# Layer 0's projections through the values' bank, and a reordered last stage, in a two-layer transformer kernel

## The chip, the cores and the metric

The kernel runs on one core of a Trainium2 chip. The metric is the device time of one execution in microseconds. A core has five engines that run their own instruction streams in order and meet through semaphores: TensorE (PE; its weight loads are shown apart as PEld), VectorE (DVE), ScalarE (ACT), GpSimd (POOL) and SyncE (SP). SP mostly issues DMAs; its queue, too, is worked in order. PSUM, into which TensorE writes, has eight banks of 128 x 512 floats.

## The reference

Two sequences of 1024 tokens with 128 features pass through two layers, all in 32-bit floats:

```python
x = x + L0_attn(layernorm(x))   # 16 heads of 64; q, k, v = z @ w @ fc + bias; softmax(q k / 8) v; out projection
x = x + L0_ffn(layernorm(x))    # 8 experts, top 2 by softmax of the router, silu(h1) * h2
x = x + L1_attn(layernorm(x))   # 16 heads of 8 with a shared rotary part of 32, causal
x = x + L1_ffn(layernorm(x))    # shared expert + 8 experts (512 wide), top 2 of a small router net
```

Layer 0's q is `(z @ wq @ fcq_w + fcq_b) / 8`, its k is `z @ wk @ fck_w + fck_b`.

## The kernel before

**PSUM.** One set of pools serves the whole kernel: two wide tiles of two banks for scores (ps_s, `wide()`), three single banks in rotation for transposes and everything else (ps_t, `bank()`), and one bank for the sums of attention values (ps_a, `acc_bank()`). A new tile of a pool waits until the last reader of the tile that had its bank is done.

**Layer 0's attention** (L387 to L640). Its order on TensorE, VectorE and ScalarE is written out by hand. The work is cut in 128 units: batch, pair of heads, block of 128 queries (eight blocks, `qt` 0 to 7, for each pair). The loop at L600 runs three units deep. In step i TensorE computes the scores of unit i (L501, four matmuls, the two heads on the two halves of the rows), transposes the probabilities of the first head of unit i-1 (L551, into two banks), adds the values of unit i-2 into ps_a (L568), and transposes the second head of unit i-1. VectorE takes maxima and moves scores to SBUF (L510), copies ps_a out when four units are summed (L575, at qt 1 and 5 of the loop), and evicts the second head's transposes (L557). ScalarE evicts the first head's transposes (L557) and takes the exponentials (L520). At qt 1 the row sums of the finished pair are transposed (L532), sent through HBM to spread them over the partitions (L538, L540, SP's queue), and GpSimd scales the outputs (L542).

The next pair's q and k are projected by `project_qk` (L473) in two halves of 512 tokens, at qt 2 and 4: two matmuls into two banks of ps_t, q evicted by VectorE (L486), k by ScalarE (L488). In steps where no projection stands and qt isn't 1, one step of other work may run: batch 1's latents, the folding of the output weights, later the routing of layer 0's experts.

At the start batch 0's layernorm runs: statistics on VectorE (L128, L129), a square root on ScalarE (L134), a reciprocal (L135) and the scaling (L153) on VectorE, then transposes, latents (L430, L435) and the first two projections. The biases bq, bk and bv are loaded by L401 on SP's queue, after x; each is 128 x 8 floats that lie apart in HBM.

**Layer 1's experts** (L897). For each batch the tokens are sorted by expert into tiles of 128 (23 tiles for batch 0; 21 for batch 1, whose last 128 tokens go through all experts). `experts1` fetches the tokens of a tile with an indirect DMA seven tiles ahead (L907), loads expert weights of 256 KB on SP's queue into four buffers (L894, issued four tiles ahead of use), and then per tile: L946 (up matmuls), L880 and L888 on VectorE with a tanh on ScalarE (L883) between them, L954 (down matmuls), L962, a scaling by the gate (L937), and an indirect store to `results` (L938). `combine1` (L1004) loads a batch's results (`z`, four DMAs on SP, L1011), which wait for all scatters of the batch, and four steps later adds them to x (L1018) and stores x.

**The last stage** (L1264 to L1284) is a list of loops over generators. When layer 1's attention is done, seven steps of batch 1's routing and sorting are left (`side`: L280 to L375 with the matmuls L289, L357, L363), eleven steps of batch 0's `experts1`, the shared expert on batch 1's first half (`half`, L1038 and L1049), and `rest` (the routing of the last token tile, L829 to L859, then the shared expert on the second half). Each loop takes one step of some of them in turn.

Of the kernel before, what the change touches and what calls it, by code (L numbers as in the profile page):

```python
# [51 lines left out]
def two_layers(ctx, tc, a, out):  # L52
# [15 lines left out]
    def bank():  # L68
        return psum["t"].tile([P, QB], F32, tag="t", name="ps_t")
# [4 lines left out]
    def load(pool, name, shape, src, eng):  # L74
        t = pool.tile(list(shape), F32, tag=name, name=name)
        eng.dma_start(out=t if len(src.shape) == 2 else t.rearrange("p (a b) -> p a b", b=src.shape[-1])
                      if len(shape) == 2 else t, in_=src)
        return t
# [308 lines left out]
    with ExitStack() as st:  # L387
# [12 lines left out]
        for k in "qkv":  # L400
            bias[k] = load(w0, f"b{k}", [P, NP], a[f"fc{k}"][D0:D0 + 1, :].rearrange("o (j p) -> p (o j)", p=P),  # L401
                           nc.sync)
        fco = load(w0, "fco", [P, NP, C], a["fco_w"].rearrange("(j p) c -> p j c", p=P), nc.scalar)
        fco_b = load(w0, "fco_b", [1, C], a["fco_b"], nc.scalar)

# [67 lines left out]
        def project_qk(b, pr, n):  # L473

            if n == 0:
                qk = a0.tile([P, 2, T], F32, tag="qk", name="qk", bufs=2)
                pairs[b, pr] = qk
            qk = pairs[b, pr]
            z, cols = lat[b][0], slice(n * QB, (n + 1) * QB)
            got = []  # L480
            for h in range(2):
                ps = bank()
                rows = slice(h * D0, (h + 1) * D0)
                nc.tensor.matmul(ps, fcqk[rows, pr * P:(pr + 1) * P], z[rows, cols], start=True, stop=True)  # L484
                got.append(ps)
            nc.vector.tensor_scalar(qk[:, 0, cols], got[0], bias["q"][:, pr:pr + 1], 1.0 / math.sqrt(D0),  # L486
                                    ALU.add, ALU.mult)
            nc.scalar.activation(qk[:, 1, cols], got[1], AF.Identity, bias=bias["k"][:, pr:pr + 1])  # L488

        units = [(b, pr, qt) for b in range(NB) for pr in range(NP) for qt in range(NT)]  # L490
        N = len(units)
# [96 lines left out]
        with tc.manual_schedule(engines={ET.PE, ET.DVE, ET.Activation}):  # L588
            lat = {}
            for _ in latents(0):  # L590
                pass
            project_qk(0, 0, 0)
            project_qk(0, 0, 1)
            wout = w0.tile([P, NP, C], F32, tag="wout", name="wout")
            extra = [latents(1), output_weights()]
            routing = route0(0, f0w, "lnT", 1, routed0[0], 1)
            temp = [lambda: a0.tile([P, T], F32, tag="pT", name="h0", bufs=6)[:, :QB],
                    lambda: a0.tile([P, T], F32, tag="p", name="o0", bufs=4)[:, :QB]]
            experts = experts0(0, routed0[0], temp)
            for i in range(N + 3):  # L600
                s = scores(i) if i < N else None
                if 1 <= i <= N:
                    probsT[i - 1] = [a0.tile([P, NT, P], F32, tag="pT", name="pT", bufs=6) for _ in range(2)]
                    evict(i - 1, 0, fill(i - 1, 0), nc.scalar.copy)
                if i < N:
                    exponentials(i, [maximum(s[0]), maximum(s[1])])
                done = units[i - 2][:2] if i >= NT and i % NT == 1 else None
                if done:
                    rs = reciprocals(done)
                if 2 <= i <= N + 1:  # L610
                    values(i - 2)
                if 1 <= i <= N:
                    evict(i - 1, 1, fill(i - 1, 1), nc.vector.tensor_copy)
                    del probs[i - 1]
                if i >= N:
                    if i == N + 1:
                        scale(done, rs)
                        for t0 in (0, TPB):
                            project_out(NB - 1, t0, TPB, range(NP - 1))
                    experts(i < N + 2)  # L620
                    continue
                b, pr, qt = units[i]
                after = (b, pr + 1) if pr + 1 < NP else (b + 1, 0)
                if after[0] < NB and qt in (2, 4):
                    project_qk(*after, qt // 2 - 1)
                if done:
                    scale(done, rs)
                if b == 0 and pr and qt not in (1, 2, 4) and extra:
                    if next(extra[0], N) == N:
                        extra.pop(0)  # L630
                        if not extra:
                            obias = output_bias()
                            for bb in range(NB):
                                nc.gpsimd.tensor_tensor(xs[bb], xs[bb], bc(obias.unsqueeze(1), [P, NT, C]), ALU.add)
                if (b, pr) == (1, 1):
                    project_out(0, qt, 1, range(NP))
                if b == 1 and pr > 1 and qt not in (1, 2, 4):
                    next(routing, None)
            for t0 in (0, TPB):
                project_out(NB - 1, t0, TPB, [NP - 1])  # L640
# [360 lines left out]
        rows = slice(t0 * P, (t0 + nt) * P)  # L1001
        nc.sync.dma_start(out=out[b, rows, :].rearrange("(t p) c -> p t c", p=P), in_=xs[b][:, t0:t0 + nt, :])

    def combine1(b, nt):  # L1004

        z = a1.tile([P, 2, NT, C], F32, tag="pT", name="z", bufs=2)
        groups = [(t0, min(TPB, nt - t0)) for t0 in range(0, nt, TPB)]
        for t0, n in groups:
            for k in range(2):
                rows = k * T + t0 * P  # L1010
                nc.sync.dma_start(out=z[:, k, t0:t0 + n], in_=results[b][rows:rows + n * P, :].rearrange("(t p) c -> p t c", p=P))  # L1011
        for _ in range(4):
            yield
        for t0, n in groups:
            yield
            xv = xs[b][:, t0:t0 + n, :]
            for k in range(2):
                nc.vector.tensor_tensor(xv, z[:, k, t0:t0 + n], xv, ALU.add)  # L1018
            store(b, t0, n)
# [34 lines left out]
    with ExitStack():  # L1054
# [122 lines left out]
        with tc.manual_schedule(engines={ET.PE, ET.DVE, ET.Activation, ET.Pool}):  # L1177
# [81 lines left out]
            def run(*steps):  # L1259

                return any([next(g, N) is None for g in steps])


            half, rest = shared1(1, 0), chain(route1(1, NT - 1, 1, "k0", "k1"), shared1(1, 1))  # L1264
            while side:
                work(N)
                run(experts) or run(half)
                run(rest)
            after = experts1(1, NT - 1, 1)
            for _ in range(AHEAD):  # L1270
                run(after)
                run(experts) or run(half) or run(rest)
            while run(experts):
                run(after)
            combining = combine1(0, NT)
            while run(after):
                run(half) or run(rest)
                run(combining)
            while run(half) or run(rest):
                pass  # L1280
            dense, combining = all_experts1(1, NT - 1), combine1(1, NT - 1)
            while run(combining, dense):
                pass
            store(1, NT - 1, 1)  # L1284
# [69 lines left out]
```

## Time and profile before

| | us |
|---|---|
| median of three runs | 1495.02 (1491.14 to 1495.07) |
| the profiled execution | 1490.81 |
| its span, first to last instruction | 1489.0 |
| busy: TensorE | 1393.7 |
| busy: VectorE | 1066.2 |
| busy: ScalarE | 885.2 |
| busy: GpSimd | 269.8 |
| L501, scores of layer 0, 1024 matmul passes | 279.9 |
| L568, values of layer 0, 4096 passes | 251.9 |
| L510, maxima of layer 0 | 303.3 |
| L520, exponentials of layer 0 | 293.1 |

A row of the timeline reads: start, length, engine, line, operation, output<-input, shape, count; in brackets the idle time of the engine just before and what ended it. A row of the waits reads: engine, its waiting instruction <- what released it: total us, times, longest us. In the slices (40 equal parts of the span, 37.2 us each) a digit is a busy share in tenths. Two TensorE passes make one matmul in 32-bit floats.

### The profile page before, as it was taken

What the parts mean: (1) busy time and instruction counts of PE and PEld (TensorE: products, weight loads), DVE (VectorE), ACT (ScalarE), POOL (GpSimd) and SP (SyncE); (2) the same over time, 40 slices, a digit from 0 to 9 for tenths busy, and PEclk for the clock granted to TensorE, in tenths of its full rate; (3) what the DMA queues carried; (4) which work ended last, traced back from release to release, by engine and by line L of the source; (5) the groups of instructions that cost most, each with busy time, mean ns of one, the idle gap of its engine ahead of it and who ended that gap; (6) DMA issues with size and microseconds to landing.
All of it is one profiled execution on the core that took longest, in us unless ns stands there. A gap on an engine that the chain in (4) does not pass through costs nothing.

```text
span 1489.0 us, 40492 instructions
## 1 busy us (share of the span) xinstructions
PE 1393.7 (94%) x16930; PEld 987.7 (66%) x16930; DVE 1066.2 (72%) x2375; ACT 885.2 (59%) x1864; POOL 269.8 (18%) x246
## 2 busy tenths in 40 slices
PE   6999999999999999999998978999988899988797
PEld 3776677777777667767765555666655567767686
DVE  4777767777766876877646558767888767878576
ACT  4667666666654676666513346876755677763443
POOL 1010001000000000000053561002111211222663
PEclk9999999999999999999999989999988999999999
DMA  4000000000000000000020030000000101112454
GB/s 110 2 16 16 16 16 9 9 16 17 16 16 1 17 16 17 16 17 4 15 49 0 1 90 2 2 2 2 2 9 9 42 25 35 47 38 53 137 135 118
DMA packets 34391, 43.15 MB, mean 29 GB/s; under 512 B 10641, under 2 KB 22578, under 8 KB 34210
## 3 DMA queue, kind: packets, MB, share of 16 engines
q1 hardware_dynamic: 28288, 28.47, 7.0%
q0 software_dynamic: 4352, 10.70, 2.7%
q8 instruction: 134, 2.20, 0.6%
q10 hardware_dynamic: 1570, 1.41, 0.4%
q14 instruction: 47, 0.39, 0.1%
HBM read 35.51 MB, written 5.05 MB: 27 GB/s over the span
## 4 chain that ended last, share of the span: by engine, by line
PE 77%; DVE 12%; ACT 6%; issue 3%; DMA 1%; POOL 0%; ACTq 0%; DVEq 0%; POOLq 0%
PE ps_a L568 16%; PE ps_s L501 15%; PE ps_t L551 10%; PE ps_s L1076 8%; PE ps_t L484 4%; PE ps_t L1118 4%; PE ps_s L253 3%; PE ps_a L1158 3%; DVE ps_s L1084 2%; PE ps_t L583 2%; ACT p L1106 2%; PE ps_t L954 2%; PE ps_t L714 2%; PE ps_t L946 1%; PE ps_t L263 1%
## 5 line engine op out<-in xcount | busy, mean ns | idle before, releaser
L510 DVE CUSTOM_DVE_ANT_0 p<-ps_s,zero 128x1024 f32<-128x1024 f32 x256 | 303.3, 1222 | 104.7 <-PE ps_s L501 104.7
L520 ACT ACTIVATE p<-p,nmx 128x1024 f32<-128x1024 f32 x256 | 293.1, 1153 | 3.0 <-DVE nmx L510 2.9
L501 PE MATMUL ps_s<-qk 64*128 64x512 f32 x1024 | 279.9, 609 | 1.5 <-DVE nmx L510 1.4
L557 ACT COPY pT<-ps_t 128x512 f32<-128x512 f32 x256 | 137.5, 589 | 211.2 <-PE ps_t L551 211.2
L568 PE MATMUL ps_a<-pT,zv 128*64 128x128 f32 x4096 | 251.9, 276 | 0.0
L551 PEld LDWEIGHTS ps_t<-ident,p 64*128 64x128 f32 x4096 | 168.1, 138 | 89.9 <-issue 86.0
L568 PEld LDWEIGHTS ps_a<-pT,zv 128*64 128x64 f32 x4096 | 221.0, 137 | 9.3 <-issue 0.8
L557 DVE COPY pT<-ps_t 128x512 f32<-128x512 f32 x256 | 164.7, 685 | 65.0 <-PE ps_t L551 65.0
L551 PE MATMUL ps_t<-ident,p 64*128 64x64 f32 x4096 | 193.7, 226 | 1.3 <-DVE pT L557 0.7
L1076 PE MATMUL ps_s<-k,qm 64*128 64x512 f32 (+3 forms) x768 | 171.2, 534 | 17.3 <-ACT p L1106 12.4
L1084 DVE CUSTOM_DVE_ANT_0 p<-ps_s,cmask 128x640 f32<-128x640 f32 (+3 forms) x128 | 125.9, 1021 | 64.8 <-PE ps_s L1076 55.6
L501 PEld LDWEIGHTS ps_s<-qk 64*128 64x128 f32 x1024 | 100.3, 188 | 84.8 <-issue 75.0
L542 POOL TENSOR_TENSOR aoT<-aoT,recip 128x1024 f32<-128x1024 f32 x16 | 37.8, 2363 | 647.2 <-DMA recip<-flat 594.2
L1118 PEld LDWEIGHTS ps_t<-ident,p 64*128 64x128 f32 x2304 | 104.1, 142 | 48.1 <-issue 23.3
L1124 ACT COPY pT<-ps_t 128x512 f32<-128x512 f32 (+3 forms) x192 | 95.9, 534 | 63.2 <-PE ps_t L1118 62.2
L1106 ACT ACTIVATE p<-p,nmx 128x640 f32<-128x640 f32 (+3 forms) x128 | 125.9, 992 | 4.3 <-DVE nmx L1084 4.2
L1076 PEld LDWEIGHTS ps_s<-k,qm 64*128 64x128 f32 x768 | 71.8, 194 | 83.4 <-issue 40.5
L1118 PE MATMUL ps_t<-ident,p 64*128 64x64 f32 x2304 | 118.0, 230 | 3.1 <-ACT pT L1124 1.3
L1158 PE MATMUL ps_a<-pT,vx 128*32 128x128 f32 x2304 | 100.0, 283 | 7.6 <-DVE pT L1124 7.5
L1124 DVE COPY pT<-ps_t 128x128 f32<-128x128 f32 (+3 forms) x192 | 87.2, 482 | 2.6 <-PE ps_t L1118 2.0
L1106 ACT ACTIVATE p<-ps_s,nmx 128x128 f32<-128x128 f32 (+3 forms) x128 | 66.5, 526 | 27.9 <-DVE nmx L1084 27.6
L1084 DVE CUSTOM_DVE_ANT_0 ps_s<-ps_s,cmask 128x128 f32<-128x128 f32 (+3 forms) x128 | 63.6, 498 | 24.7 <-PE ps_s L1076 19.9
(245 smaller groups left out, 1779.1 us busy)
## 6 DMA issues: line engine op xcount, KB each, us to landing
we<-in_we SPq DMA_DIRECT2D x52, 256.0 KB, 2.7
recip<-flat SPq DMA_DIRECT2D x32, 256.0 KB, 3.9
we<-in_we POOLq DMA_DIRECT2D x1, 2048.0 KB
z<-results SPq DMA_DIRECT2D x6, 256.0 KB, 4.0
x<-in_x SPq DMA_DIRECT2D x4, 256.0 KB, 3.9
up<-in_up_proj POOLq DMA_DIRECT2D x1, 1024.0 KB, 12.1
normed<-y SPq DMA_DIRECT2D x3, 256.0 KB, 2.3
out_x<-x SPq DMA_DIRECT2D x3, 256.0 KB
```

Source lines behind the costliest of these rows:

```text
L501: nc.tensor.matmul(s[h][:, n * QB:(n + 1) * QB], qk[rows, 0, qt * P:(qt + 1) * P], qk[rows, 1, n * QB:(n + 1) * QB], start=True, stop=True)
L510: nc.vector.tensor_tensor_reduce(p, s, bc(zero, [P, T]), -1.0, 3e38, ALU.add, ALU.min, nmx)
L520: nc.scalar.activation(p, p, AF.Exp, bias=nmx, scale=-1.0, accum_out=ssum[:, h, qt:qt + 1])
L551: nc.tensor.transpose(ps[r][:, k * 64:(k + 1) * 64], probs[i][h][rows, k * P:(k + 1) * P], ident[rows, rows])
L557: copy(probsT[i][h][:, :, r * 64:(r + 1) * 64], ps[r].rearrange("p (j q) -> p j q", q=64))
L568: nc.tensor.matmul(acc[h * D0:(h + 1) * D0, cols], zv[:, j, :], probsT[i][h][:, j, :], start=(j == 0), stop=(j == NT - 1))
L1076: nc.tensor.matmul(s[h][:, n * QB:n * QB + w], qms[b, qt][rows, pr, :], kTs[b][pr // 4][rows, n * QB:n * QB + w], start=True, stop=True)
L1084: nc.vector.tensor_tensor_reduce(to[:, :nk], s[:, :nk], cmask[:, T - nk:], -1.0, 3e38, ALU.add, ALU.min, nmx)
L1106: nc.scalar.activation(p[:, h, :nk], s[h][:, :nk], AF.Exp, bias=nmx[h], scale=-1.0, accum_out=sums[b, qt][:, head:head + 1])
L1118: nc.tensor.transpose(ps[r][:, c * 64:(c + 1) * 64], probs[i][rows, h, j * P:(j + 1) * P], ident[rows, rows])
L1124: copy(probsT[i][:, 8 * f:8 * f + n, r * 64:(r + 1) * 64], ps[r][:, :n * 64].rearrange("p (j q) -> p j q", q=64))
L1158: nc.tensor.matmul(acc[to * 32:(to + 1) * 32, k * P:(k + 1) * P], vx[:, j, g, pr % 4 * 24:pr % 4 * 24 + 32], probsT[i][:, h * (qt + 1) + j ...
```

## The change

The change has three parts. `project_qk` puts q into ps_a and k into ps_t, both evictions go to ScalarE (q's with the scale 1/8 as an immediate and a bias that is scaled once at the start, `scaled_bq`), and projections stand at qt 1 and 5, so that other work may use six of eight steps. `combine1` can wait a number of steps before it loads. In the last stage, the loop over `side` takes a step of batch 0's experts only every second time and no step of `half`; the loop of seven fetches alternates `half` and batch 0's experts; batch 0's last experts then alternate with batch 1's first steps; and batch 0's combining waits six steps.

```diff
+        scaled_bq = w0.tile([P, NP], F32, tag="scaled_bq", name="scaled_bq")
+        nc.vector.tensor_scalar(scaled_bq, bias["q"], 1.0 / math.sqrt(D0), None, ALU.mult)
         fco = load(w0, "fco", [P, NP, C], a["fco_w"].rearrange("(j p) c -> p j c", p=P), nc.scalar)
...
-            got = []
+            got = [acc_bank(), bank()]
             for h in range(2):
-                ps = bank()
                 rows = slice(h * D0, (h + 1) * D0)
-                nc.tensor.matmul(ps, fcqk[rows, pr * P:(pr + 1) * P], z[rows, cols], start=True, stop=True)
-                got.append(ps)
-            nc.vector.tensor_scalar(qk[:, 0, cols], got[0], bias["q"][:, pr:pr + 1], 1.0 / math.sqrt(D0),
-                                    ALU.add, ALU.mult)
-            nc.scalar.activation(qk[:, 1, cols], got[1], AF.Identity, bias=bias["k"][:, pr:pr + 1])
+                nc.tensor.matmul(got[h], fcqk[rows, pr * P:(pr + 1) * P], z[rows, cols], start=True, stop=True)
+            for h, (scale, add) in enumerate(((1.0 / math.sqrt(D0), scaled_bq), (1.0, bias["k"]))):
+                nc.scalar.activation(qk[:, h, cols], got[h], AF.Identity, bias=add[:, pr:pr + 1], scale=scale)
...
-                if after[0] < NB and qt in (2, 4):
-                    project_qk(*after, qt // 2 - 1)
+                if after[0] < NB and qt in (1, 5):
+                    project_qk(*after, qt // TPB)
                 if done:
                     scale(done, rs)
-                if b == 0 and pr and qt not in (1, 2, 4) and extra:
+                if b == 0 and pr and qt not in (1, 5) and extra:
...
-                if b == 1 and pr > 1 and qt not in (1, 2, 4):
+                if b == 1 and pr > 1 and qt not in (1, 5):
                     next(routing, None)
...
-    def combine1(b, nt):
+    def combine1(b, nt, wait):
+        for _ in range(wait):
+            yield
         z = a1.tile([P, 2, NT, C], F32, tag="pT", name="z", bufs=2)
...
+            k = 0
             while side:
                 work(N)
-                run(experts) or run(half)
+                if k % 2 == 0:
+                    run(experts)
                 run(rest)
+                k += 1
             after = experts1(1, NT - 1, 1)
-            for _ in range(AHEAD):
+            for k in range(AHEAD):
                 run(after)
-                run(experts) or run(half) or run(rest)
+                run(half) if k % 2 else run(experts)
             while run(experts):
                 run(after)
-            combining = combine1(0, NT)
+            combining = combine1(0, NT, 6)
             while run(after):
                 run(half) or run(rest)
                 run(combining)
             while run(half) or run(rest):
                 pass
-            dense, combining = all_experts1(1, NT - 1), combine1(1, NT - 1)
+            dense, combining = all_experts1(1, NT - 1), combine1(1, NT - 1, 0)
```

## The prediction

> **What bounds the kernel now.** I read the page's first two parts first, to see which engine is full in which stage.
>
> ```profile
> PE 1393.7 (94%) x16930; PEld 987.7 (66%) x16930; DVE 1066.2 (72%) x2375; ACT 885.2 (59%) x1864; POOL 269.8 (18%) x246
> PE   6999999999999999999998978999988899988797
> PEclk9999999999999999999999989999988999999999
> ```
>
> Layer 0's attention fills the first half: TensorE is in the nines, at full clock. A microsecond taken from TensorE's order there should come off the end. The 37th slice shows a hole (7). Next, one unit without and one with a projection, from the timeline:
>
> ```profile
> 206.35 1.97 PE L568 MATMUL ps_a<-pT,zv 128*64 128x128 f32 x32
> 208.25 0.71 PE L551 MATMUL ps_t<-ident,p 64*128 64x64 f32 x16
> 208.53 0.63 DVE L575 COPY aoT<-ps_a 128x512 f32<-128x512 f32 x1
> 208.88 0.28 PE L532 MATMUL ps_t<-ident,rs 128*16 128x128 f32 x1
> 209.07 1.27 DVE L557 COPY pT<-ps_t 128x512 f32<-128x512 f32 x2
> ...
> 211.50 1.97 PE L568 MATMUL ps_a<-pT,zv 128*64 128x128 f32 x32
> 213.88 0.30 PEld L484 LDWEIGHTS ps_t<-zqk,fcqk 64*128 64x128 f32 x2
> 214.14 1.29 DVE L557 COPY pT<-ps_t 128x512 f32<-128x512 f32 x2 [0.54 <-PE ps_t L551]
> 214.88 0.18 PEld L484 LDWEIGHTS ps_t<-zqk,fcqk 64*128 64x128 f32 x1 [0.70 <-DVE pT L557]
> 218.14 0.96 PEld L568 LDWEIGHTS ps_a<-pT,zv 128*64 128x64 f32 x18
> ```
>
> From one value group (L568) to the next a plain unit takes 4.80 us everywhere in this stage. The unit with L532 takes 5.15 (206.35 to 211.50), a unit with a projection 6.64 (211.50 to 218.14; the others 6.65). So a projection costs 1.85 us, though its q and k matmuls use different row halves. The last bracket says why: k's bank is one that the transposes have just filled, and its weight load waits 0.70 us for VectorE's eviction. The list of waits for 40 to 740 us has 20.2 us of this, 29 times.
>
> The end of the kernel, from the waits of the DMA queue and the table by stretches (columns: stretch, length, busy of PE, PEld, DVE, ACT, POOL, granted clock, DMA share, GB/s):
>
> ```profile
> SPq L1011 <- DMA results<-o,s_to: 14.3, 1, 14.3
> ```
>
> ```profile
> 1404.00:1408.00 4.00, 0.25 (x3) 0.01 (x1) 1.49 (x3) 1.11 (x3) 3.09 (x4) 1.00 1.05 258
> 1408.00:1412.00 4.00, 2.21 (x10) 2.25 (x11) 0.13 (x1) 0.00 (x0) 1.52 (x2) 0.53 0.66 241
> 1412.00:1416.00 4.00, 4.00 (x25) 4.00 (x24) 0.85 (x2) 1.20 (x3) 0.99 (x1) 0.62 0.24 66
> ```
>
> SP stands 14.3 us at batch 0's result load, which needs the last scatter; behind it in SP's order waits batch 1's fourth weight load. Issued at last at 1403.19, behind 1 MB of results, it lands just before 1409.79, and TensorE idles 5.54 us. Then the clock is at half.
>
> **The change, part by part.** (1) Projections. q goes to the value bank ps_a, k to the third transpose bank, at units 1 and 5. Walk through the unit at 206 to 211: transposes issue until 208.88. k's bank was last emptied by ScalarE's eviction ahead of the exponentials (done 207.5): free. q needs L575's copy, done 209.16: a wait of 0.3 us. At unit 5 the reciprocal before L575 is absent, so I take 0.2. Then the pair of matmuls. The first projections (18.1 us) show what a pair without a bank wait does: k's and q's evictions start 0.04 us apart, so the halves run together. Score weight loads (the same shape, both halves) advance 0.43 us per pair of passes; a projection pair has two: 0.86. So 1.85 becomes 1.16 and 1.06. With 15 later pairs of heads: 15 x (3.70 - 2.22) = 22.2 us saved.
>
> L532 now stands behind the projection at unit 1. It takes the bank of the second transposes' first half, evicted by 209.71; it is reached at about 210.0: no wait. Its three DMAs (L538, L540 twice) go out about 1.2 us later. The gpsimd multiply behind them has 46 us of idle before it (its row at 216.26), and SP has nothing else here: nothing. The q eviction moves from VectorE (0.74) to ScalarE (0.69, row of L488), 32 times: ScalarE has 3.9 us of work in a plain unit and 5.1 in this one, which takes TensorE about 6.3. ps_a is free again by 211.0 and the next values come after 212.5: hidden. If that cover were gone, each microsecond of ScalarE lateness would be a microsecond at the values. Batch 1's latents and the routing get six slots per head pair instead of five: the same instructions, earlier, no gain.
>
> (2) Start. The new multiply scaled_bq sits in VectorE's order between the last statistics (7.14) and the reciprocal, and it waits for the bq load.
>
> ```profile
> 3.68 0.37 SPq L76 DMA_DIRECT2D bq<-in_fcq  x1
> 5.12 5.64 SPq L76 DMA_DIRECT2D bv<-in_fcv  x1
> ...
> 10.56 0.20 DVE L135 RECIPROCAL rstd<-rstd 128x8 f32<-128x8 f32 x1 [3.24 <-ACT rstd L134]
> ```
>
> Before, nobody needed bq until 19.24. Here a rule speaks against the change. The Trainium skill, DMA: Bandwidth & Descriptors, section "Latency and other measured facts", puts a DMA's fixed cost at about 2 us; by that bq is there at 5.7 and the multiply costs nothing. But its "Rules for kernel authors" say that a non-contiguous last dimension becomes one descriptor per element, and bq is 1024 single floats. The nearest row is bv, the same shape: landed 14.1 us after issue, at 19.2. bq is issued 1.4 us earlier; the trace's landing events for its semaphore run from 10.45 to 16.72. I take 16.72: everything after the reciprocal (layernorm, transposes, latents, first projections) slides from 10.56 to about 16.9, +6.3 us. Ends: 0 (the page) and +8.8 (bv's landing). Also the first four evictions now queue on ScalarE alone: k's second half ends about 22.5 instead of 21.9, +0.6. Sum +6.9.
>
> (3) End. Batch 0's last three experts now alternate with batch 1's first; the result loads come in the seventh step of combining, by which time SP has issued seven weight loads and the last scatter is near. Removed: the idle of 5.54 us, and the cold stretch after it: L946 at 1409.79 to the next at 1416.07 takes 6.28 us where the same four groups later take 3.68 (1446.82 to 1450.50), so 2.6. Of the drain at 1387 to 1402 (TensorE idle 0.95, 1.01, 0.67 and 0.78) 3.4. Together 11.5.
>
> Added: with experts in only every second step, batch 1's routing chain loses cover. L357 still waits for place_hot (0.6), L363 for the copy of L357 (0.45), and L852 for ScalarE's L843, queued behind a tanh (1.6); in their place 1.8 of old idle goes: +0.9. Would these gaps cool TensorE? The Trainium skill, TensorE: Matmul & The Clock Gate, section "What's actually happening", wants an idle window of about 3.4 us: then nothing. The trace disagrees: after waits of 1.58 and less the granted clock falls to 0.50 at 1364 to 1366, which costs some 1.8 us against warm steps; after the gap at 1379 it stays 1.00. I take +1.0 (0 to 1.8). Result loads and weight loads meet on the queue later; the stall may reappear in part: +0.5 (0 to 3). Combining itself (four adds, two stores) only moves inside the loop over batch 1's experts. Net of (3): -9.1.
>
> Sum: -22.2 + 6.9 - 9.1 = -24.4. The profiled execution took 1490.81 (span 1489.0): 1466.4. The three runs have their median 4.2 above it, at 1495.02, which gives 1470.6; between the two I forecast **1468**.
>
> **Rivals.**
> - Only the projections pay: the stall at the end moves behind the later result loads, or into the thinner routing steps. For it: SP keeps one order, and 1 MB of results still has to come in. Against it: seven weight loads are then ahead. About 1477.
> - bq lands before the reciprocal wants it: 6.3 better, 1462. Against it: the landing events.
> - The pair does not overlap (1.72 for 0.86): the projections then save 15 x (3.70 - 3.94), a loss of 3.6; 1494, no change. Against it: the two evictions 0.04 us apart at the start.
> - Slower: ps_a as a new wait. One bank now serves values and q, so TensorE waits for L575 before q and for ScalarE before the next values. If exponentials ran late, q's eviction would hold that bank. Against it: about 1.5 us of slack in the walk above. It decides once the added wait at each of 30 projections passes (24.4 + 4.5) / 30 = 1.0 us; at 1.3 us the kernel stands near 1507.
>
> **How the numbers follow.** 0.3% (4.5 us) is about what can be told from no change. Forecast as summed: 0.68; projections only: 0.14; early bq: 0.09; no overlap: 0.04; slower: 0.05. Faster takes the first three, 0.91; same 0.04; slower 0.05. Range: the terms allow 6 us either way on the projections, +2 to -6 at the start, 5 either way at the end, and 2 for the base; with the second and third cases inside it, 1456 to 1482.
>
> **What would show it.** Units 1 and 5 between value groups at 6.3 and 5.9 us, units 2 and 4 at 4.80, and no wait of L486's on L557. The reciprocal near 16.9 with VectorE idle for the bq load before it. No idle of TensorE for weights near batch 1's fourth expert and no long wait of SP at the result load. I am wrong if units 1 and 5 stay above 6.6, if the start doesn't slip, or if TensorE's idle in the last 125 us isn't smaller.

## The result

The changed kernel takes 1471.87 us, the median of four runs (1469.89 to 1473.5). The kernel before, run beside it, takes 1494.82 us (1491.14 to 1495.07). The ratio is 0.9852, with a 95% interval of 0.9829 to 0.9874: faster by 22.95 us. The forecast was 1468, its range 1456 to 1482, and the sum behind it -24.4 us.

The size is nearly right, but not because each term was. One part paid less than worked out, one cost more, and one paid more. The first two parts of the page after show the frame: TensorE is busy for 23.7 us less (1393.7 before), ScalarE has 18.7 us more (885.2) and VectorE 20.4 us less (1066.2), since q's eviction changed engines.

```profile
PE 1370.0 (93%) x16930; PEld 977.9 (66%) x16930; DVE 1045.8 (71%) x2344; ACT 903.9 (61%) x1896; POOL 271.0 (18%) x246
PE   3999999999999999999998988999998899988997
PEclk9999999999999999999999979999978999999999
```

The number of matmul passes is the same, so 23.7 us less "busy" is not less work. It comes from passes that no longer stand in line behind a wait (L501 alone is busy for 254.5 us where it was 279.9), and from passes that run at a higher clock at the end. The first slice has a 3 where there was a 6: the start got worse. The hole (a 7 before) is a 9; it is in the 38th slice, where the prediction says the 37th. Since a profile is one execution, it has to be said where it stands among the runs: the profile before is of a run of 1490.81, one of its quickest, and the profile after of one of 1473.5, the slowest of its four. Their spans, 1489.0 and 1471.7, differ by only 17.3 us. The other 5.6 us of the 22.95 are which executions were profiled: the first lies 4.0 under its median, the second 1.6 over.

This table cuts the spans at rows that both traces have. "Start" ends with the start of the first maximum (L510), "attention" is from the first values (L568) of layer 0 to the last, "middle" from there to the last output projection of layer 1's attention (L1172, L1174 after), and "end" from there to the last down matmul of the experts (L954).

| us | before | after | after - before |
|---|---|---|---|
| reciprocal (L135) starts | 10.56 | 18.95 | +8.4 |
| first maximum starts | 23.23 | 32.76 | +9.5 |
| layer 0's attention | 705.00 | 690.98 | -14.0 |
| middle (not touched) | 622.92 | 622.25 | -0.7 |
| end | 101.98 | 89.02 | -13.0 |
| from one value group to the next, unit 1 | 5.16 | 6.54 | +1.38 |
| the same, unit 5 | 4.80 | 6.03 | +1.23 |
| the same, units 2 and 4 | 6.65 | 4.80 | -1.85 each |

**Start.** The timeline of the changed kernel (start, length, engine, line, operation, output<-input; in brackets the idle time before it and what ended that):

```profile
3.76 0.37 SPq L76 DMA_DIRECT2D bq<-in_fcq  x1
...
11.82 0.30 ACT L134 ACTIVATE rstd<-bnmv,eps_col 128x8 f32<-128x8 f32 x1
18.87 0.17 DVE L404 TENSOR_SCALAR scaled_bq<-bq 128x8 f32<-128x8 f32 x1 [11.47 <-DMA bq<-in_fcq]
18.95 0.20 DVE L135 RECIPROCAL rstd<-rstd 128x8 f32<-128x8 f32 x1
```

VectorE stands idle for 11.47 us at a multiply of 0.17 us. The square root that the reciprocal needs was done by 12.1. bq, 4 KB, took 15.1 us from issue to use. Nothing of the kernel needs scaled_bq before 27 us; what needs VectorE is the reciprocal behind it. Of the 9.5 us at the first maximum some 1 us can be the execution: e2 and e6 below, whose start is that of the kernel before, have their first maximum at 23.89 and 24.61 where this profile of before has 23.23.

**Projections.** The waits of TensorE at the projections' matmuls from 40 to 740 us (total us, times, longest), first the row of before (there the line is L484), then that of the changed kernel (L486):

```profile
PEld ps_t L484 <- DVE pT L557: 20.2, 29, 0.7
```

```profile
PE ps_a L486 <- DVE aoT L575: 7.2, 29, 0.6
```

The 20.2 us of waits for VectorE's eviction of the transposes (L557) are gone from the projections; in their place TensorE waits for the copy of the value sums (L575), 7.2 us in 29 projections. One unit 1 from the timeline, and the projection of the unit 5 that follows it:

```profile
80.75 0.25 DVE L525 RECIPROCAL rs<-ssum 128x16 f32<-128x16 f32 x1
80.92 0.63 DVE L575 COPY aoT<-ps_a 128x512 f32<-128x512 f32 x1
81.46 1.27 DVE L557 COPY pT<-ps_t 128x512 f32<-128x512 f32 x2
81.60 0.69 PE L486 MATMUL ps_a<-zqk,fcqk 64*128 64x512 f32 x1 [0.41 <-DVE aoT L575]
81.61 0.69 PE L486 MATMUL ps_t<-zqk,fcqk 64*128 64x512 f32 x1
82.14 0.59 PE L486 MATMUL ps_a<-zqk,fcqk 64*128 64x512 f32 x1
82.66 0.28 PE L532 MATMUL ps_t<-ident,rs 128*16 128x128 f32 x1
...
102.61 0.69 PE L486 MATMUL ps_a<-zqk,fcqk 64*128 64x512 f32 x1 [0.30 <-DVE aoT L575]
```

q and k start 0.01 us apart: the two row halves run together. From the first pass to what follows the pair it is 1.06 us here (81.60 to 82.66), and 0.96 in unit 5, where the scores start at 103.57. The bracket differs from pair to pair (0.15 to 0.60), since the end of a matmul is modelled; the intervals between value groups hardly differ, and are what the sum should be made from.

**End.** The table by stretches (columns: stretch, length in us, busy of PE, PEld, DVE, ACT, POOL with counts, granted clock, DMA share, GB/s) over the stage's whole length. Before:

```profile
1361.00:1463.00 102.00, 85.72 (x639) 77.28 (x640) 67.91 (x160) 44.94 (x114) 55.33 (x54) 0.95 0.47 130
1364.00:1366.00 2.00, 2.00 (x11) 2.00 (x11) 1.95 (x6) 0.24 (x1) 0.98 (x1) 0.50 0.18 27
```

After:

```profile
1357.00:1446.00 89.00, 80.38 (x641) 73.04 (x640) 67.34 (x159) 44.81 (x114) 56.58 (x54) 1.00 0.52 148
```

The same 640 weight loads. TensorE's idle time fell from 102 - 85.72 = 16.3 us to 89 - 80.38 = 8.6, by 7.7; and its busy time fell by 5.3, while the mean granted clock rose from 0.95 to 1.00. Both cold stretches of before are gone here, the one behind the stall at 1404 and the one at 1364. But only the first is the change's doing. e2 below has the same last stage, and there the second stands as before:

```profile
1362.38:1450.82 88.44, 81.60 (x641) 74.59 (x640) 67.37 (x159) 44.72 (x114) 57.11 (x54) 0.98 0.53 150
1366.00:1368.00 2.00, 2.00 (x12) 2.00 (x11) 2.00 (x6) 0.00 (x0) 0.62 (x1) 0.50 0.61 164
```

Yet the stage takes no more time there: 88.4 us. So the split into 7.7 and 5.3 is that of one execution; in e2 the idle time fell by 9.4 and the busy time by 4.1. The stall of before in TensorE's rows (idle time in brackets), and below it the gaps of the changed kernel's stage that bear on the forecast:

```profile
1409.79 2.05 PE L946 MATMUL ps_t<-xT,we 128*128 128x128 f32 x8 [5.54 <-DMA we<-in_we]
```

```profile
1363.24 1.16 PE L954 MATMUL ps_t<-we,h 128*128 x8 [1.25 <-DVE h L880]
...
1368.04 0.25 PE L363 MATMUL ps_t<-ident,atT 42*128 42x42 f32 x1 [0.35 <-ACT atT L360]
...
1371.74 0.41 PE L852 MATMUL ps_t<-lnT,wr 128*32 128x128 f32 x2 [1.21 <-ACT lnT L843]
...
1408.20 1.13 PE L946 MATMUL ps_t<-xT,we 128*128 128x128 f32 x8 [0.93 <-DMA we<-in_we]
```

The 5.54 us for weights are now 0.93, because SP issues batch 0's result loads at 1398.85, late enough that the longest of its waits for scattered results in the whole stage, both batches', is 3.9 us instead of 14.3:

```profile
SPq L1013 <- DMA results<-o,s_to: 7.6, 3, 3.9
```

### The profile page after: what moved, and what is told of

It is laid out like the page before. It is cut to its first block, busy times and chain, and to the rows that moved or that the text cites. A ratio compares the mean times of both kernels' runs of the same rounds, so it can differ in the third digit from the quotient of the medians.

```text
span 1471.7 us, 40504 instructions
## 1 busy us (share of the span) xinstructions
PE 1370.0 (93%) x16930; PEld 977.9 (66%) x16930; DVE 1045.8 (71%) x2344; ACT 903.9 (61%) x1896; POOL 271.0 (18%) x246
## 4 chain that ended last, share of the span: by engine, by line
PE 71%; DVE 16%; ACT 5%; issue 5%; DMA 2%; POOL 0%; SPq 0%; DVEq 0%; POOLq 0%; ACTq 0%
PE ps_s L501 15%; PE ps_a L568 13%; PE ps_s L1078 8%; PE ps_t L551 8%; PE ps_t L1120 4%; PE ps_s L253 3%; PE ps_a L1160 3%; DVE p L510 3%; PE ps_a L486 2%; DVE ps_s L1086 2%; PE ps_t L583 2%; ACT p L1108 2%; PE ps_t L954 2%; PE ps_t L946 2%; PE ps_t L714 2%
## 5 line engine op out<-in xcount | busy, mean ns | idle before, releaser
L510 DVE CUSTOM_DVE_ANT_0 p<-ps_s,zero 128x1024 f32<-128x1024 f32 x256 | 303.4, 1222 | 136.9 <-PE ps_s L501 136.0
L557 ACT COPY pT<-ps_t 128x512 f32<-128x512 f32 x256 | 137.5, 589 | 196.5 <-PE ps_t L551 196.5
L501 PE MATMUL ps_s<-qk 64*128 64x512 f32 x1024 | 254.5, 611 | 3.4 <-DVE nmx L510 2.9
L568 PE MATMUL ps_a<-pT,zv 128*64 128x128 f32 x4096 | 251.9, 276 | 0.0
L568 PEld LDWEIGHTS ps_a<-pT,zv 128*64 128x64 f32 x4096 | 220.9, 137 | 9.4 <-issue 0.8
L551 PEld LDWEIGHTS ps_t<-ident,p 64*128 64x128 f32 x4096 | 159.7, 139 | 90.9 <-issue 83.3
L557 DVE COPY pT<-ps_t 128x512 f32<-128x512 f32 x256 | 164.7, 685 | 53.8 <-PE ps_t L551 53.8
L551 PE MATMUL ps_t<-ident,p 64*128 64x64 f32 x4096 | 177.4, 226 | 1.3 <-DVE pT L557 0.7
L542 POOL TENSOR_TENSOR aoT<-aoT,recip 128x1024 f32<-128x1024 f32 x16 | 37.9, 2368 | 641.0 <-DMA recip<-flat 536.1
L501 PEld LDWEIGHTS ps_s<-qk 64*128 64x128 f32 x1024 | 91.0, 188 | 81.1 <-issue 69.1
L1120 PEld LDWEIGHTS ps_t<-ident,p 64*128 64x128 f32 x2304 | 104.8, 143 | 47.3 <-issue 23.1
L1120 PE MATMUL ps_t<-ident,p 64*128 64x64 f32 x2304 | 118.3, 231 | 2.4 <-ACT pT L1126 1.3
```

Source lines behind the costliest of these rows:

```text
L501: nc.tensor.matmul(s[h][:, n * QB:(n + 1) * QB], qk[rows, 0, qt * P:(qt + 1) * P], qk[rows, 1, n * QB:(n + 1) * QB], start=True, stop=True)
L510: nc.vector.tensor_tensor_reduce(p, s, bc(zero, [P, T]), -1.0, 3e38, ALU.add, ALU.min, nmx)
L551: nc.tensor.transpose(ps[r][:, k * 64:(k + 1) * 64], probs[i][h][rows, k * P:(k + 1) * P], ident[rows, rows])
L557: copy(probsT[i][h][:, :, r * 64:(r + 1) * 64], ps[r].rearrange("p (j q) -> p j q", q=64))
L568: nc.tensor.matmul(acc[h * D0:(h + 1) * D0, cols], zv[:, j, :], probsT[i][h][:, j, :], start=(j == 0), stop=(j == NT - 1))
L1120: nc.tensor.transpose(ps[r][:, c * 64:(c + 1) * 64], probs[i][rows, h, j * P:(j + 1) * P], ident[rows, rows])
```

## The experiments

Ten kernels were run, in three groups. Kernels of a group share a chip and the runs of the kernel before. As that kernel's median differs a little between groups (1492.63, 1492.67 and 1492.13; 1494.82 beside the change), "gain" is against the kernel before of the same group. The stages are as above, each from one profiled execution.

| kernel | median us | ratio [95%] | gain | first maximum | attention | middle | end | unit 1 | unit 5 |
|---|---|---|---|---|---|---|---|---|---|
| the change | 1471.87 | 0.9852 [0.9829, 0.9874] | 22.9 | 32.76 | 691.0 | 622.3 | 89.0 | 6.54 | 6.03 |
| e1_projections_alone | 1485.05 | 0.9943 [0.9924, 0.9962] | 7.6 | 31.84 | 691.0 | 625.4 | 102.5 | 6.54 | 6.03 |
| e2_last_stage_alone | 1479.76 | 0.9917 [0.99, 0.9933] | 12.9 | 23.89 | 705.0 | 622.2 | 88.4 | 5.16 | 4.80 |
| e3_bias_later | 1464.89 | 0.982 [0.9804, 0.9837] | 27.7 | 24.58 | 691.1 | 621.8 | 88.6 | 6.54 | 6.03 |
| e4_q_on_vector | 1462.99 | 0.9821 [0.9791, 0.9851] | 29.6 | 24.45 | 690.3 | 619.2 | 91.0 | 6.54 | 6.03 |
| e5_old_banks | 1489.73 | 0.9976 [0.9959, 0.9993] | 2.9 | 32.17 | 708.4 | 625.4 | 88.9 | 7.12 | 6.65 |
| e6_wait_alone | 1484.66 | 0.9944 [0.9928, 0.9961] | 8.0 | 24.61 | 705.0 | 622.8 | 94.0 | 5.16 | 4.80 |
| e7_no_wait | 1473.53 | 0.9881 [0.9865, 0.9898] | 19.1 | 30.04 | 691.0 | 618.5 | 91.1 | 6.54 | 6.03 |
| e8_copy_first | 1465.06 | 0.9819 [0.9802, 0.9835] | 27.6 | 25.48 | 688.9 | 621.2 | 88.5 | 6.44 | 6.03 |
| e9_bias_first | 1461.19 | 0.9802 [0.9783, 0.9821] | 30.9 | 23.02 | 690.6 | 618.9 | 88.6 | 6.54 | 6.03 |
| e10_vector_copy_first | 1465.56 | 0.9817 [0.9802, 0.9832] | 26.6 | 25.00 | 687.8 | 628.0 | 89.4 | 6.44 | 6.03 |

### The two halves of the change, each alone

e1 is the kernel before with the projections' part (banks, evictions, scaled_bq, places) and the old last stage:

```diff
+        nc.vector.tensor_scalar(scaled_bq, bias["q"], 1.0 / math.sqrt(D0), None, ALU.mult)
...
+            got = [acc_bank(), bank()]
...
-                if after[0] < NB and qt in (2, 4):
+                if after[0] < NB and qt in (1, 5):
```

> The kernel before with the projections' part alone (ps_a for q, third bank for k, ScalarE for both, units 1 and 5, scaled_bq at the start); the last stage as before. My theory: value-group intervals of 6.54 us at unit 1 and 6.03 at unit 5, 4.80 at units 2 and 4, which saves 15 x 1.08 = 16 us; the start gives back 9 to 10 us (reciprocal near 17 to 19 us, waiting for the bq load); sum -6 to -8 us, so about 1487. From L1172's last to L954's last start 102 us as before. Rival (the projections pay for everything, the last stage nothing): -22, about 1473.

e2 is the kernel before with `combine1`'s wait and the new loops of the last stage alone:

```diff
-                run(experts) or run(half)
+                if k % 2 == 0:
+                    run(experts)
...
-                run(experts) or run(half) or run(rest)
+                run(half) if k % 2 else run(experts)
...
-            combining = combine1(0, NT)
+            combining = combine1(0, NT, 6)
```

> The kernel before with the last stage's part alone (order of the loops, combining that waits six steps). My theory: the stretch from L1172's last to L954's last goes from 102 to 89 us, -13; nothing else changes; about 1482. TensorE waits under 1.5 us for expert weights (5.5 before) and SP under 5 us at the first result load (14.3 before). Rival (projections pay for everything): no change, about 1495.

Measured: 7.6 us for e1 and 12.9 for e2. Together 20.5, against 22.95 for the whole: they add up, within what two differences of medians can tell. So by the medians the larger part of the net gain comes from the last stage, since the late start eats half of what the projections save. By its units e1 should gain 7.7: units 1 and 5 cost 1.38 + 1.23 more, units 2 and 4 save 2 x 1.85, so 1.09 per pair of heads and 15 x 1.09 = 16.3 us; its first maximum is 8.6 later (31.84 against 23.23). That this meets 7.6 so well is in part luck: its attention stage as a whole fell by 14.0, not 16.3, and 14.0 - 8.6 is 5.4. The rival by which only the projections pay is refuted.

### What the late bias costs

e3 is the changed kernel with the multiply moved behind batch 0's latents in VectorE's order, just ahead of the first projection:

```diff
-        nc.vector.tensor_scalar(scaled_bq, bias["q"], 1.0 / math.sqrt(D0), None, ALU.mult)
...
             for _ in latents(0):
                 pass
+            nc.vector.tensor_scalar(scaled_bq, bias["q"], 1.0 / math.sqrt(D0), None, ALU.mult)
             project_qk(0, 0, 0)
```

> The changed kernel with the instruction scaled_bq moved behind batch 0's latents in VectorE's order, ahead of the first projection. My theory: the reciprocal comes near 10.6 to 12 us again, the first maximum near 24 to 26 instead of 32.8; 7 to 9 us off the changed kernel, about 1463 to 1465. Rival (the start slips because four evictions stand on ScalarE, or because a table load is late): under 2 us off.

e4 has no scaled_bq; q is evicted by VectorE as before, but still from ps_a:

```diff
-        nc.vector.tensor_scalar(scaled_bq, bias["q"], 1.0 / math.sqrt(D0), None, ALU.mult)
...
-            for h, (scale, add) in enumerate(((1.0 / math.sqrt(D0), scaled_bq), (1.0, bias["k"]))):
-                nc.scalar.activation(qk[:, h, cols], got[h], AF.Identity, bias=add[:, pr:pr + 1], scale=scale)
+            nc.vector.tensor_scalar(qk[:, 0, cols], got[0], bias["q"][:, pr:pr + 1], 1.0 / math.sqrt(D0),
+                                    ALU.add, ALU.mult)
+            nc.scalar.activation(qk[:, 1, cols], got[1], AF.Identity, bias=bias["k"][:, pr:pr + 1])
```

> The changed kernel with q's eviction back on VectorE as one instruction (add, then multiply) out of ps_a, without scaled_bq; the bank of q and the units stay. My theory: the bank is what frees TensorE, not the engine that evicts: value-group intervals at units 1 and 5 stay within 0.3 us of 6.54 and 6.03, and the start is free of the wait for bq; 7 to 10 us off the changed kernel, about 1463. Rival (moving q's eviction off VectorE is what pays): units 1 and 5 grow by 0.7 us or more each, +20 us on the attention stage, so slower than the changed kernel by 10.

e9 leaves the multiply where the change has it, and has bq loaded first on SP's queue, ahead of x:

```diff
+    early_bq = const.tile([P, H0 // 2], F32, tag="early_bq", name="early_bq")
+    nc.sync.dma_start(out=early_bq, in_=a["fcq"][D0:D0 + 1, :].rearrange("o (j p) -> p (o j)", p=P))
     xs = []
...
-        bias = {}
-        for k in "qkv":
+        bias = {"q": early_bq}
+        for k in "kv":
```

> The changed kernel with one DMA moved: bq is loaded ahead of x on SP's queue, into a tile of its own; scaled_bq stays at the start, now ahead of the statistics in VectorE's order. If bq is late because its 1024 single floats share the sixteen DMA engines with the 3.5 MB of other loads, it lands within 2 to 4 us here, the statistics begin near 4 to 5 us, the reciprocal stands at 11 to 13 us, and the time is that of e3_bias_later, about 1465. Rival (such a load takes some 14 us by itself): the statistics don't begin before 14 us, and the time is 1472 or more.

All three take the first maximum back by 8.2 to 9.7 us (24.58, 24.45 and 23.02 against 32.76). In time they are 7.0, 8.9 and 10.7 us under the change's median; with each set against the kernel before of its own group, it is 4.8, 6.7 and 8.0. e3's timeline:

```profile
11.86 0.20 DVE L135 RECIPROCAL rstd<-rstd 128x8 f32<-128x8 f32 x1 [4.40 <-ACT rstd L134]
18.98 0.17 DVE L591 TENSOR_SCALAR scaled_bq<-bq 128x8 f32<-128x8 f32 x1 [1.00 <-DMA bq<-in_fcq]
```

The load is no quicker (18.98), but what waits with it is now only the projection, and VectorE's idle time before the multiply is 1.00 us. e9's timeline (its lines stand two further down than those of the change):

```profile
0.74 0.43 SPq L82 DMA_DIRECT2D early_bq<-in_fcq  x1
3.24 0.17 DVE L406 TENSOR_SCALAR scaled_bq<-early_bq 128x8 f32<-128x8 f32 x1 [2.24 <-DMA early_bq<-in_fcq]
10.23 0.20 DVE L137 RECIPROCAL rstd<-rstd 128x8 f32<-128x8 f32 x1 [0.90 <-ACT rstd L136]
```

Here the same 1024 single floats are used 2.5 us after their issue, and x isn't visibly later for it: the reciprocal starts at 10.23. So the pattern of single floats does not by itself make the load slow. Among the loads that are in flight at 4 to 18 us it takes 15.1, as the first of its queue 2.5. Whether the 12.6 us between them go to x ahead of it on SP's queue or to the loads of the other two queues, these runs don't separate.

e9 is the quickest kernel of the study: 1461.19 us (1459.24 to 1466.16), 0.9802 of the kernel before. It beats the change as well; its interval lies wholly below the change's. It overlaps those of e3, e4, e8 and e10.

### Bank or place, and who evicts

e5 is the changed kernel with q back in a bank of ps_t, at the new places (units 1 and 5):

```diff
-            got = [acc_bank(), bank()]
+            got = [bank(), bank()]
```

> The changed kernel with q and k both in the transposes' banks again; units 1 and 5, ScalarE for both evictions and the last stage stay. My theory (the bank is what pays): k's matmul waits for VectorE's eviction again, 0.7 us or more for each projection, since at these units that eviction stands behind the copy of ps_a; units 1 and 5 rise to about 7.1 and 6.7 us, some 15 to 20 us on the attention stage, about 1488. Rival (the choice of units and the engine pay): units 1 and 5 within 0.3 us of 6.54 and 6.03, time as the changed kernel, about 1472.

Units 1 and 5 become 7.12 and 6.65 us: with units 2 and 4 at 4.80 a pair of heads has 23.37 us in them, against 23.26 before. The place alone is worth nothing; the attention stage as a whole is even 3.4 us longer than before (708.4 against 705.0). The bank is worth 0.58 + 0.62 = 1.20 per pair of heads, 18.0 in all, where attention is 17.4 us longer than the change's and the gain falls from 22.9 to 2.9. e5's weight loads show the old wait, in the list for 40 to 740 us and in one unit's rows:

```profile
PEld ps_t L486 <- DVE pT L557: 22.9, 30, 1.1
```

```profile
84.35 0.30 PEld L486 LDWEIGHTS ps_t<-zqk,fcqk 64*128 64x128 f32 x2
84.41 2.29 PE L486 MATMUL ps_t<-zqk,fcqk 64*128 64x512 f32 x4
84.85 1.27 DVE L557 COPY pT<-ps_t 128x512 f32<-128x512 f32 x2
85.58 0.29 PEld L486 LDWEIGHTS ps_t<-zqk,fcqk 64*128 64x128 f32 x2 [0.92 <-DVE pT L557]
```

q's weights are loaded at 84.35, k's at 85.58, after 0.92 us of waiting for the bank that L557 empties: the two halves run one after the other. (e5's 13 runs spread from 1484.19 to 1496.76, wider than the others', the longer ones mostly at a lower mean granted clock: 0.984 at 1484.19, 0.973 at 1496.76; its profile is of the slowest. The units are read within one execution and don't hang on that.)

e4, above, answers the other question: with q's eviction on VectorE again, from ps_a, the units stay at 6.54 and 6.03. The engine of the eviction is worth nothing here; the scaled bias was made for ScalarE's eviction, so the price at the start bought nothing.

e8 is e3 with the value copy (L575, in `values`) ahead of the reciprocal (L525) in VectorE's order, to shorten the new wait in unit 1:

```diff
-                if done:
-                    rs = reciprocals(done)
                 if 2 <= i <= N + 1:
                     values(i - 2)
+                if done:
+                    rs = reciprocals(done)
```

> As e3_bias_later, and at unit 1 the copy of ps_a stands ahead of the reciprocals of the row sums in VectorE's order. My theory: q's wait for ps_a shrinks by the 0.17 us between the two starts at each of 15 units; unit 1 at 6.37, attention 2.5 us shorter, about 1462. Rival (L532 needs the reciprocals at once and waits instead): unit 1 stays at 6.54 or grows.

e10 is e4 with the same reorder (q evicted by VectorE, no scaled bias).

> The two best variants together: q's eviction on VectorE out of ps_a without scaled_bq, and the copy of ps_a ahead of the reciprocals. My theory: unit 1 at 6.44 as in e8_copy_first, reciprocal near 11, about 1461 to 1463. Rival (the evictions on VectorE and the earlier copy stand in each other's way): unit 1 at 6.54 or more, 1463 or more.

Unit 1 falls from 6.54 to 6.44 us in both, so the reciprocal's place accounts for 0.10 of it; attention is 2.2 us shorter in e8 than in e3 and 2.5 shorter in e10 than in e4. In time nothing is to be seen: 1465.06 beside e3's 1464.89, and 1465.56 beside e4's 1462.99. In e10's profiled execution the middle, which no edit touches, took 628.0 us where it took 619.2 in e4's; that hides the gain in that execution. Its mean granted clock there is 0.95, against 0.97 in e4's; e1 and e5, which don't have the reorder, show the same 0.95 and 625.4 us. So the reorder isn't needed for such a middle. As an improvement e8 and e10 are inconclusive.

### Wait or order, at the end

e6 is the kernel before with the six steps of waiting in `combine1` and no other change:

```diff
-            combining = combine1(0, NT)
+            combining = combine1(0, NT, 6)
```

> The kernel before with one thing of the last stage changed: batch 0's combining waits six steps before it loads. My theory: SP is no longer held at the result load, the idle of 5.5 us and the cold stretch of 2.6 us after it go, the drain of batch 0's experts stays: stretch from L1172 to L954 at about 94 us (102 before), -8, about 1485. Rival (the order of the loops is what pays): no change.

The end takes 94.0 us instead of 102.0, and the gain is 8.0. The waits of e6's last stage:

```profile
PE ps_t L946 <- DMA we<-in_we: 1.6, 1, 1.6
```

```profile
SPq L1013 <- DMA results<-o,s_to: 12.5, 1, 12.5
```

and SP's timeline:

```profile
1382.83 6.44 SPq L894 DMA_DIRECT2D we<-in_we  x4
1402.13 1.48 SPq L1013 DMA_DIRECT2D z<-results  x3
1404.23 0.36 SPq L894 DMA_DIRECT2D we<-in_we  x1
```

SP still stands 12.5 us at a result load. That is nearly the 14.3 of before, but four of batch 1's weight loads are now ahead of it in SP's order instead of three (1381.63 to 1386.29 before), and TensorE, which gets to the fifth later than it got to the fourth, idles 1.6 us for weights instead of 5.5. A long wait on SP's row means little by itself; what counts is what was issued before it.

e7 is the changed kernel without the wait:

```diff
-            combining = combine1(0, NT, 6)
+            combining = combine1(0, NT, 0)
```

> The changed kernel with batch 0's combining loading at once; the order of the loops stays. My theory: the result load stands in SP's queue before the last scatters have landed, batch 1's next weight load waits behind it, and TensorE stands still for some 5 to 7 us with a cold stretch behind it: stretch from L1172 to L954 at 95 to 99 us (89), 1478 to 1482. Rival (with the new order the last scatters are early enough): as the changed kernel, 1472.

The end takes 91.1 us, 2.1 more than the change's; the gain is 19.1 instead of 22.9. By time alone the two aren't told apart: the intervals of their ratios overlap, and e7's profiled execution began 2.7 us earlier (first maximum at 30.04). That the stall would come back without the wait is refuted. e7's timeline, of GpSimd, SP and TensorE:

```profile
1389.61 0.97 POOL L938 DMA_INDIRECT results<-o,s_to  x1 [0.30 <-issue]
...
1391.99 2.03 SPq L1013 DMA_DIRECT2D z<-results  x4
1394.26 7.18 SPq L894 DMA_DIRECT2D we<-in_we  x5
...
1399.95 1.13 PE L946 MATMUL ps_t<-xT,we 128*128 128x128 f32 x8 [1.74 <-DMA we<-in_we]
```

Batch 0's last scatter goes out at 1389.61, and the result loads follow 2.4 us later. In the kernel before, that scatter went out at 1398.43, the first result load at 1400.92 and the next weights at 1403.19. In the new order SP issues seven of batch 1's weight loads from 1371.93 to 1384.54, ahead of those result loads; before, it had issued three when it came to stand. So either edit removes most of the stall: 8.0 by the wait alone, 10.9 in the end stage by the order alone (102.0 - 91.1), 13.0 by both. They overlap; the wait adds about 2 to the new order.

## Why the prediction was right, and where it was not

The signs, the mechanism of each part and the total held; the total in part by luck, since each term was off. The terms, in the order of the prediction:

| us | predicted | measured | from |
|---|---|---|---|
| projections | -22.2 | -16.3 | 15 x (23.26 - 22.17), the units 1, 2, 4 and 5 of one pair of heads |
| start | +6.9 | +9.5 | first maximum, 23.23 to 32.76 |
| end | -9.1 | -13.0 | 101.98 to 89.02 |
| sum | -24.4 | -19.8 | the three above |

**Projections, mechanism right, the pair mis-sized.** "Units 1 and 5 at 6.3 and 5.9": they are 6.54 and 6.03; units 2 and 4 at 4.80 and the missing wait for L557 came as said. The step that failed is "a projection pair has two: 0.86", taken from score weight loads that advance 0.43 us per pair of passes. Measured from the pair's first pass to its follower it is 1.06 in unit 1 and 0.96 in unit 5. In unit 1 q's two passes stand 0.54 apart (81.60 to 82.14), and what follows comes 0.52 after the second; the score loads are a running stream, while these start out of a wait. What fills the 0.1 each isn't shown. The wait for L575 had been put at 0.3 and 0.2. By the rows it is about 0.3 in both: q's first pass starts 2.86 us after the value group in unit 1 (120.29 to 123.15), where L532 came after 2.53 before (206.35 to 208.88), and 2.76 in unit 5 (58.14 to 60.90), where scores start after 2.45 in a plain unit (90.08 to 92.53). So unit 1 was set 0.23 too low, nearly all of it the pair's, and unit 5 0.17, half the pair's and half the wait's; 15 x 0.40 is the difference. The stage as a whole fell by 14.0, 2.3 less than the units account for. Here a term failed that had been put at nothing: "the same instructions, earlier, no gain". The fourth and fifth pairs of heads of batch 1, which carry most of the routing, took 90.08 us together before and 92.13 after, where a pair without other work fell by 1.07 (42.47 to 41.40). One row of the routing shows why: before, and then after.

```profile
605.65 0.23 DVE L192 TENSOR_TENSOR r_h<-r_eq,r_k 128x64 f32<-128x64 f32 x1
```

```profile
581.31 2.36 POOL L542 TENSOR_TENSOR aoT<-aoT,recip 128x1024 f32<-128x1024 f32 x1 [43.64 <-DVE r_eq L189]
581.72 2.03 DVE L192 TENSOR_TENSOR r_h<-r_eq,r_k 128x64 f32<-128x64 f32 x1
584.94 2.70 PE L501 MATMUL ps_s<-qk 64*128 64x512 f32 x7 [1.43 <-DVE nmx L510]
```

With projections at units 1 and 5 the routing may stand in unit 2, and there it meets GpSimd's multiply: VectorE's row of 0.23 us takes 2.03, the maxima behind it are late, and TensorE waits 1.43 us for them. In all nine profiles with the new places one such row of the routing takes 2.0 to 2.4 us beside L542; in the three with the old places (before, e2, e6) none does. No run moves the multiply away, so that it is what holds VectorE is read from these rows, not tested, and the rest of the loss in these pairs is open.

e5 shows the bank as the cause, and the slower rival's point (1.0 us of added wait per projection) was far off: the longest wait is 0.6.

**Start, mechanism right, both terms too small.** "I take 16.72", the last landing event of bq before; in the profile after it is 18.85, and in the profiles of e1, e5 and e7, which have the same wait, the reciprocal starts at 17.98, 19.13 and 17.28. The landing is no constant of the kernel, and the ends given, 0 and +8.8, were the honest bounds: +8.4 came out near the upper one. The Trainium skill's fixed cost of about 2 us (DMA: Bandwidth & Descriptors, "Latency and other measured facts") is not wrong: in e9 the load took 2.5. It is not what a load takes that stands behind others, 15.1 us here, and the row of its neighbour in the same crowd was the better guide. Behind the reciprocal another 1.1 us was lost. 0.5 of it is between the first projections and the maximum (18.08 to 23.23 before, 27.09 to 32.76 after). That is near the +0.6, but its reason, four evictions on ScalarE, doesn't suffice: e5 has the same four and takes 5.09 us there, against 5.15 before and 5.66 in the change. In the change the second half's q also waits for its one bank, until ScalarE has emptied it:

```profile
28.99 0.69 PE L486 MATMUL ps_a<-zqk,fcqk 64*128 64x512 f32 x1 [0.77 <-ACT qk L488]
```

It takes both, the one bank and ScalarE: e4, with the bank but VectorE's eviction, takes 5.19. The other 0.6 is in the latents, whose L432 takes 3.41 us to the next group (21.85 to 25.26) where it took 2.78 before. It need not be the change's: from the reciprocal to the first projection it is 7.51 us before and 8.14 after, but 8.02 and 7.42 in e2 and e6, which have the old start.

**End, mechanism right, the clock mis-sized.** The prediction's idle terms are 5.54 + 3.4 taken away and 0.9 + 0.5 added: 7.5 us. Its cold terms are 2.6 taken away and 1.0 added: 1.6. In the profile after it is 7.7 and 5.3; but there the old cold stretch of the routing steps is missing, which e2 has. With e2 it is 9.4 and 4.1. The step that failed is "I take +1.0 (0 to 1.8)": the thinner routing steps cooled nothing beyond what had been cold, 0 in place of 1.0. The old stretch had been left in the sum as it stood, rightly. In e2, e3, e8 and e9 it is there and the stage takes 88.4 to 88.6 us; in the change, e5 and e10 it is not, and the stage takes 88.9 to 89.4; so it costs the stage nothing that shows. What the stall took with it beyond 5.54 + 2.6, about 3 us, is not traced to rows. Of the single gaps, L357 has none (0.6 predicted), L363 0.35 (0.45), L852 1.21 (1.6).

**The sum.** The measured terms make -19.8. The profiles' spans differ by -17.3: the 2.3 that attention gained less, 0.8 between the first maximum and the first values, and -0.7 of the middle. Against the -24.4 that is 7.1 short. The medians differ by -22.95, because the profile before is of a quick execution and the profile after of the slowest. Too much on the projections (5.9) and too little at the start (2.6) were nearly met by too little at the end (3.9): a nearly right total of three mis-sized terms, and luck to that extent. The prediction put its base between the profile's own time and the median, 4.2 us above it; the median of before came out at 1494.82, and from there the sum gives 1470.4, where 1471.87 was measured.

The named rivals: "bq lands before the reciprocal wants it, 1462" is not what the change does, but it is what e9 does, at 1461.19. "The pair does not overlap" is refuted by the starts 0.01 us apart.

## What to carry to other kernels

An instruction of 0.17 us is not free when it stands in an engine's order ahead of work that is due and waits for a DMA: look up when its operand lands, in the trace of this kernel and beside these neighbours, and put it behind that work, or the load ahead of its queue. When matmuls on two row halves are to run together, both output banks must be free at that moment: ask for each bank who emptied it last, and when. For a wait on a DMA queue, ask what has been issued ahead of it, not how long it is; and expect that two edits which shorten the same stall won't add up. When slots come free and other work moves into them, look up what runs on the other engines beside it there.

## What the hardware showed unexpectedly

The same load of 1024 single floats took 2.5 us from issue to use at the head of its queue (e9) and 15.1 us behind x and beside the loads of two other queues (the change).

The granted clock did not follow the gaps. In the routing steps of the last stage every kernel has the same gap of 1.58 us ahead of L946. Behind it the clock fell to 0.50 before and in e2 (1364 to 1366 and 1366 to 1368 us), and in e3, e4, e6, e7, e8 and e9 as well; in the change, e1, e5 and e10 it stayed at 1.00. e1 has the old last stage, e2 the new one, so it isn't the order of the stage either. A rule by the length of a single gap explains none of this; the runs don't show what does.

A VectorE instruction of the routing on 128 x 64 floats took 2.03 us where GpSimd's multiply of 2.36 us ran beside it (the change), and 0.23 where it didn't (before).

The middle of the kernel, 620 us that none of these edits touches, took 618.5 to 628.0 us in the profiled executions, and its mean granted clock goes with that: 0.95 in the three longest (625.4, 625.4 and 628.0), 0.96 or 0.97 in the others (618.5 to 622.9). Differences of under some 5 us between variants (e3, e4, e8 and e10 among themselves) are therefore not told apart here.
